# An x product of an LSTM's input stream on the whole TensorE array instead of on its four column quarters

## The chip, the cores and the metric

The kernel runs on one core of one Trainium2 chip. A core has five engines that work side by side: PE (TensorE, the 128x128 matmul array, with its weight loads listed apart as PEld), DVE (VectorE), ACT (ScalarE), POOL (GpSimd) and SP (SyncE, which here issues transfers). The metric is the device time of one execution in microseconds (us), lower is better; it is given as the median of several runs. Beside it stands the profile of one execution, whose span runs from the first to the last instruction.

## The reference, cut to what matters

```python
x = x + lstm(x, h0=cond_1024, Wx, Wh, b)          # x: (32, 512, 512) = batch, steps, features

xW = jnp.einsum('ntd,dg->ntg', x, Wx) + b          # Wx: (512, 2048)
c = 0
for each of the 512 steps:
    a = xW[:, t] + prev_h @ Wh                     # Wh: (512, 2048)
    i, f, o = sigmoid(a[:, :H]), sigmoid(a[:, H:2H]), sigmoid(a[:, 2H:3H])
    g = tanh(a[:, 3H:])                            # H = 512
    next_c = f * prev_c + i * g
    next_h = o * tanh(next_c)
```

Everything is 32-bit float. There are two kinds of matrix work: x times Wx, which depends on no step before it, and h times Wh, of which step t needs the h of step t-1.

## The kernel before, in words

**The recurrent product.** In a step, `h_part` multiplies h (32 batch rows, held transposed in four pieces of 128x32) by Wh. The 32 batch rows are the stationary operand, so one matmul fills only 32 of the array's 128 columns. Four matmuls, one for each quarter j of the hidden units, are therefore put on the four column quarters of the array, each with the same 128x32 piece of h and its own 512 columns of Wh, writing partitions 32j to 32j+31 of a bank of PSUM (`gbank`). With four pieces of h that is 16 matmuls a step. The steps up to 468 are done so; after that the banks are split in halves and no part of the stream is left.

**The stream of x products.** For steps 18 to 497, x times Wx is done ahead of time, in 15 groups of 32 steps, by a fast matrix multiplication scheme of two levels: 26 products of sums of blocks (the slots of a group), each again split into 7 products (Winograd's form of Strassen's scheme). So there are 15 x 26 x 7 = 2730 *x products*. One x product has a left operand of 128x128 (x, or sums of blocks of x, in `ubuf`, `xs0` or the tile `r1`) and a right operand of 128x256 (sums of blocks of Wx, mostly in `vring`, which is loaded again and again from DRAM), and it adds a 128x256 result to a bank of PSUM (`xbank` or `bbank`). ACT and DVE take the results out to `cbuf` and add them up, and SP stores them to DRAM, from where each step loads its own row (`xw`).

`emit_matmuls` issues the x products. Before the change it cuts the left operand into four pieces of 32 columns and issues four matmuls, one on each column quarter, all with the same right operand. A call gets a number n of quarter products that are due; when fewer than four are left, it issues half a product (128 of the 256 columns), and the next call the other half.

**Other matmuls.** The first 18 steps and a few at the end have their x times Wx done plainly (`plain_block`, `plain_part`, `Tail.matmuls`), with 128x32 stationary operands on the column quarters. At the very beginning eight bf16 matmuls with 128x128 operands of zeros open the banks.

**What sets the order.** All instructions from step 20 on, and those before it in a first piece, are collected by `Plan`, which keeps PE's instructions in program order (recurrent product of step t, then the x products due in step t, then the recurrent product of step t+1) and simulates the other engines with a table of costs (`Plan.cost`) to choose the order in which DVE, ACT, POOL and SP issue theirs. `cell` does the gates on ACT and DVE between two recurrent products: sigmoids and tanh, the products, the new cell, its tanh, the new h, and its transpose into `ht`, which the next `h_part` waits for. All instructions are recorded through one helper, so every row of the profile has its line, L127; rows are told apart by their tiles.

Names in the rows: `gbank<-wh_sb,ht` is the recurrent product, `xbank` or `bbank` `<-vring,ubuf` (or `r`, `xs`, `cbuf` and others on the right) an x product. "128*32" is the part of the array that an instruction uses, rows by columns. A 32-bit matmul shows as two records in the trace, each with a weight load of its own: the 16 matmuls of a recurrent product are 32 records, an x product on the quarters 8.

Of the kernel before, what the change touches and what calls it, by code (L numbers as in the profile page):

```python
# [14 lines left out]
P = 128  # L15
B = 32
# [6 lines left out]
W = G * P  # L23
# [60 lines left out]
RIGHT = {1: 0, 5: 1, 3: 2, 6: 3, 2: 4, 7: 5, 4: 6}  # L84
# [22 lines left out]
class Plan:  # L107
# [70 lines left out]
    def cost(self, engine, op, out, ins):  # L178
        n = self.columns(out)
        if engine == "PE":  # L180
            need = (n * 4 / 2.4 + 5.26) / 4
            return need, need + self.PE_DEPTH
        if engine == "DVE":
            if op == "memset":
                return n, n
            took = 178 + 1.04 * n if op == "transpose" else 155 + 1.04 * n
            return took - 80, took
        if engine == "ACT":
            took = (185 + 0.78 * n) if op == "activation" else (150 + 0.86 * n)
            return max(took - 120, 105.0), took  # L190
        if engine == "POOL":
            return 478.0, 478.0
        return 430.0, 0.0
# [19 lines left out]
    def flush(self):  # L213
# [23 lines left out]
        cost = [self.cost(o[0], o[1], o[3], o[4]) for o in ops]  # L237
        moved = [self.dma_time(o[3], o[4][0]) if "dma" in o[1] else (0, 0.0, "") for o in ops]
        horizon = sum(c[0] for c, o in zip(cost, ops) if o[0] == "PE")
        late = [0.0] * n  # L240
        after = horizon
        for i in range(n - 1, -1, -1):
# [6 lines left out]
            if e == "PE":  # L249
                v = min(v, after - cost[i][0])  # L250
                after = v
            late[i] = v
        self.problem = ops, preds, succs, cost, moved
        order, ready = self.listed(late)
        for move in MOVES:
# [14 lines left out]
    def shaken(self, late, seed, lo, hi, spread, engines):  # L270
# [4 lines left out]
        ]  # L275

    def simulate(self, ops, preds, succs, cost, moved, late, expect):
        n = len(ops)
        engines = ("PE", "DVE", "ACT", "POOL", "SP")
# [110 lines left out]
def kernel(  # L390
# [11 lines left out]
    nc = Plan(tc.nc)  # L402
# [278 lines left out]
    def group(g):  # L681
        if g not in groups:
            groups[g] = Group(g)
        return groups[g]
# [105 lines left out]
    def u_block(gr, i):  # L790
        if i < 2 * MB:
            q = XROWS.index(i // 2)
            assert gr.summed[q] == 4, (gr.g, i)
            return pairs_at(PLACES[gr.g % 2][q])[:, i % 2]
        return None
# [32 lines left out]
    def left_of(gr, s, r):  # L828
        b = u_block(gr, U_OF[s])
        return ubuf[:, gr.u[U_OF[s]], LEFT[r]] if b is None else b[:, 1 + LEFT[r]]  # L830

    def left_done(gr, s):
        u_used(gr, U_OF[s])
# [47 lines left out]
    def emit_matmuls(n):  # L881

        while n > 0 and pos[0] < 4 * len(items):
            i, q = divmod(pos[0], 4)
            row, slot, r = items[i]
            gr, s = group(slot // R), slot % R
            xb = xbank[slot % 5]
            if q == 0 and any(f in finished for f in needs(slot, r)):
                if wait_at_end[0]:
                    return  # L890
                evacuate()
            if r == 2:
                dst = bbank[:, slot % 2 * HW : (slot % 2 + 1) * HW]
            elif r in (5, 3):
                dst = xb[:, HW:W]
            else:
                dst = xb[:, 0:HW]
            start = q == 0 and (r == 2 or (r == 1 and s not in BIAS_OF))
            size = 4 if q == 0 and n >= 4 else 2
            cols = slice(q * HW // 4, (q + size) * HW // 4)  # L900
            for j in range(4):
                nc.tensor.matmul(
                    dst[j * B : (j + 1) * B, cols],
                    left_of(gr, s, r)[:, j * B : (j + 1) * B],
                    right_of(row, slot, RIGHT[r])[:, cols],
                    start=start,
                    stop=True,
                    skip_group_check=True,
                )
            pos[0] += size  # L910
            n -= size
            if pos[0] % 4 == 0:
                finished.append((slot, r))
                if r == 4:
                    left_done(gr, s)
                    if slot < HELD:
                        (free_u if slot == 1 else free_c).extend({1: (6, 7), 2: (V_OF[2],), 3: (V_OF[3],)}.get(slot, ()))

    def right_of(row, slot, k):
        if slot >= HELD:  # L920
            return vring[:, row % 3, k]
        return v_parts(V_OF[slot])[2] if k == 6 else v_parts(V_OF[slot])[k % 2][:, k // 2]

    def needs(slot, r):
        if r == 1:
            return ((slot - 5, 4),)
        if r == 2:
            return ((slot - 2, 2),)
        return {5: (), 6: ((slot, 5),), 3: ((slot, 5),), 7: ((slot, 3),), 4: ((slot, 7),)}[r]
# [29 lines left out]
    def evacuate():  # L959
        while wqueue and len(free_c) < sum(r == 5 for _, r in finished):  # L960
            w_op(True)
        for slot, r in finished:
            gr, s = group(slot // R), slot % R
            xb = xbank[slot % 5]
            if r == 5:
                gr.have[s, "c"] = take(free_c)
                t = buf_of(gr.have[s, "c"])
                nc.scalar.copy(t[:, 0:4:3], xb.rearrange("p (n c) -> p n c", n=2))
                continue
            if r in (1, 6):  # L970
                continue
            t = buf_of(gr.have[s, "c"])
            if r == 2:
                add(t[:, 0], bbank[:, slot % 2 * HW : (slot % 2 + 1) * HW], t[:, 0])
                room["dve"] -= cost_dve(256)
            elif r == 3:
                nc.scalar.copy(t[:, 1], xb[:, 0:HW])
                add(t[:, 1], xb[:, HW:W], t[:, 1])
                room["dve"] -= cost_dve(256)
            elif r == 7:  # L980
                add(t[:, 3], xb[:, 0:HW], t[:, 3])
                room["dve"] -= cost_dve(256)
            else:
                nc.scalar.copy(t[:, 2], xb[:, 0:HW])
                gr.have[s] = gr.have.pop((s, "c"))
                ready(gr, s)
        finished.clear()
# [92 lines left out]
    def v_parts(i):  # L1080
        if i < 8:
            return r1[:, i, 1:4], r2[:, i, 0:3], r2[:, i, 3]
        return split_parts(vroom[vt[i]])
# [318 lines left out]
    with tc.manual_schedule():  # L1402
# [8 lines left out]
        for q in range(2):  # L1411
            cols = slice(q * P, (q + 1) * P)
            nc.sync.dma_start(out=r1[:, 0:4, 1, cols], in_=first[:, :, 1, cols])
        nc.sync.dma_start(out=r1[:, 0:4, 0], in_=first[:, :, 0])
        for c in range(1, 4):
            ko, ki = divmod(c, 2)
            if c == 1:
                load_early(1, 1, 2)
            nc.sync.dma_start(
                out=r1[:, 4 * ko : 4 * ko + 4, 2 * ki : 2 * ki + 2].rearrange("p j s c -> p j (s c)"),  # L1420
# [5 lines left out]
            out=wh_sb[:, k].rearrange("p j c -> p (j c)"), in_=wh[:, k * NJ * W : (k + 1) * NJ * W]  # L1426
# [60 lines left out]
        for t in range(T):  # L1487
# [19 lines left out]
            if HEAD + 4 <= t < HEAD + 4 + 3 * len(V_DIRECT):  # L1507
                s, d = divmod(t - HEAD - 4, 3)
# [15 lines left out]
            if t < HEAD_STEPS:  # L1524
# [22 lines left out]
                for i, (kind, m, cs) in enumerate(chunks):  # L1547
# [16 lines left out]
                    else:  # L1564
# [22 lines left out]
                        if i == 0 and t + 1 in SEEDED and t + 1 != HEAD:  # L1587
                            seed_step(t + 1)
                        emit_matmuls(m)
                        room["dve"] += m * PROD / 4  # L1590
                        if i == late_cell:
# [21 lines left out]
            n = target  # L1613
# [19 lines left out]
            if t in LATE:  # L1633
                late_loads.pop(0)()
            emit_matmuls(n)
            load_v_ahead()
            if t == SPLIT - 1:
# [73 lines left out]
```

## Time and profile before

| | |
|---|---|
| time, median of 3 runs | 3058.33 us (3058.26 to 3058.35) |
| profiled execution: span from first to last instruction | 3056.5 us |
| what lies around the span | about 1.8 us, if the profiled execution took the median time |
| PE busy | 3050.1 us (100%), 43424 records |
| PEld busy | 1605.6 us (53%), 43424 records |
| DVE busy | 2362.2 us (77%) |
| ACT busy | 1479.6 us (48%) |
| POOL busy | 222.9 us (7%) |
| mean share of the 16 DMA engines | 75.5% in the main queue |
| granted TensorE clock | 1.000 |

The page does not give the profiled execution a time of its own apart from its span; 1.8 us is the difference to the median. A matmul's record begins when PE takes it up and its end is modelled, so records of successive matmuls overlap; how long PE needs for one is read from the distance between the starts of successive ones. A row of the timeline merges successive records of one kind: its start, the time to the end of the last of them, and their count. Busy time of an engine is the time covered by any of its records. Idle time stands with what ended it.

### The profile page before, as it was taken

How to read it: one execution, taken by the hardware profiler on the slowest of the kernel's cores; microseconds unless marked ns; L12 is line 12 of the kernel's file. 1: busy time of each engine (PE TensorE's matmuls, PEld its weight loads, DVE VectorE, ACT ScalarE, POOL GpSimd, SP SyncE). 2: the span in 40 equal slices, each digit the busy share in tenths (PEclk: the TensorE clock that was granted, in tenths of full speed). 3: DMA queues.
4: the chain of work that ended last, by engine and by line, in shares of the span. 5: the costliest groups of instructions: out<-in, count | busy, mean ns of one | idle time of the engine just before them, and what ended most of it. 6: DMA issues, size and time to landing. Idle time of an engine off the chain costs nothing.

```text
span 3056.5 us, 107859 instructions
## 1 busy us (share of the span) xinstructions
PE 3050.1 (100%) x43424; PEld 1605.6 (53%) x43424; DVE 2362.2 (77%) x6518; ACT 1479.6 (48%) x5511; POOL 222.9 (7%) x473
## 2 busy tenths in 40 slices
PE   9999999999999999999999999999999999999999
PEld 6774444444444555555555555555555555555666
DVE  8678787787878878787787877878778787787765
ACT  2345445454444544545445454454544545444554
POOL 0000000000000000000000000000000000000000
PEclk9999999999999999999999999999999999999999
DMA  9889877787877778778787787877777778788630
GB/s 352 288 281 291 265 255 256 236 265 231 273 242 248 260 237 268 247 239 273 228 271 237 245 267 238 264 242 250 256 246 252 250 250 262 244 259 273 206 98 20
DMA packets 321428, 753.92 MB, mean 247 GB/s; under 512 B 51104, under 2 KB 106400, under 8 KB 320416
## 3 DMA queue, kind: packets, MB, share of 16 engines
q1 hardware_dynamic: 320784, 747.02, 75.5%
q8 instruction: 342, 5.60, 0.8%
q14 instruction: 158, 1.29, 0.1%
q10 hardware_dynamic: 144, 0.01, 0.0%
HBM read 565.68 MB, written 184.29 MB: 245 GB/s over the span
## 4 chain that ended last, share of the span: by engine, by line
PE 99%; DVE 0%; DMA 0%; ACT 0%; issue 0%; SPq 0%; DVEq 0%
PE gbank L127 56%; PE xbank L127 38%; PE bbank L127 6%; DMA r<-in_L_cond_Wx_dram 0%; DVE prod L127 0%; ACT s L127 0%; DVE s L127 0%; SPq L127 0%; DVE hbuf L127 0%; DVE ht L127 0%; ACT tanh_c L127 0%; ACT vring L127 0%; DVE vring L127 0%; ACT cbuf L127 0%; ACT r L127 0%
## 5 line engine op out<-in xcount | busy, mean ns | idle before, releaser
L127 PE MATMUL gbank<-wh_sb,ht 128*32 128x512 f32 x14912 | 1695.2, 592 | 0.3
L127 PEld LDWEIGHTS gbank<-wh_sb,ht 128*32 128x32 f32 x14912 | 537.9, 110 | 820.9 <-issue 713.0
L127 ACT ACTIVATE s<-gbank 128x64 f32<-128x64 f32 (+2 forms) x1920 | 331.2, 257 | 1209.6 <-PE gbank L127 1208.0
L127 PE MATMUL xbank<-vring,ubuf 128*32 128x256 f32 (+1 forms) x13584 | 848.0, 368 | 0.0
L127 PEld LDWEIGHTS xbank<-vring,ubuf 128*32 128x32 f32 x13584 | 512.6, 110 | 305.6 <-issue 137.5
L127 DVE TENSOR_TENSOR prod<-s 128x128 f32<-128x128 f32 (+2 forms) x1093 | 296.9, 278 | 469.4 <-ACT s L127 464.8
L127 POOL TENSOR_TENSOR oc<-xnat,ht 128x128 f32<-128x128 f32 x469 | 222.7, 475 | 2642.7 <-DVE ht L127 1292.1
L127 ACT ACTIVATE tanh_c<-s 128x64 f32<-128x64 f32 (+1 forms) x921 | 236.8, 258 | 190.0 <-DVE s L127 185.7
L127 ACT COPY cbuf<-xbank 128x256 f32<-128x256 f32 (+1 forms) x696 | 289.2, 439 | 38.7 <-PE xbank L127 34.0
L127 ACT COPY gbank<-xw 128x512 f32<-128x512 f32 (+1 forms) x486 | 285.2, 589 | 0.2
L127 DVE STREAM_TRANSPOSE ht<-hbuf 128x64 f32<-128x64 f32 (+1 forms) x921 | 226.9, 246 | 65.1 <-DVE hbuf L127 1.8
L127 DVE TENSOR_TENSOR s<-prod 128x64 f32<-128x64 f32 (+1 forms) x1007 | 227.4, 226 | 34.1
L127 DVE TENSOR_TENSOR cbuf<-xbank,cbuf 128x256 f32<-128x256 f32 x462 | 180.8, 409 | 46.3 <-ACT cbuf L127 42.6
L127 DVE TENSOR_TENSOR cbuf<-cbuf 128x1024 f32<-128x1024 f32 x172 | 209.5, 1222 | 0.6
L127 PE MATMUL xbank<-vring,r 128*32 128x256 f32 (+1 forms) x3216 | 207.5, 357 | 0.0
L127 PE MATMUL xbank<-vring,xs 128*32 128x256 f32 (+1 forms) x3120 | 200.9, 356 | 0.0
L127 DVE TENSOR_TENSOR hbuf<-o,tanh_c 128x64 f32<-128x64 f32 (+1 forms) x921 | 190.2, 207 | 3.7 <-ACT tanh_c L127 3.4
L127 ACT COPY r<-xbank 128x256 f32<-128x256 f32 (+1 forms) x414 | 176.3, 439 | 15.7 <-PE xbank L127 13.8
L127 PE MATMUL bbank<-vring,ubuf 128*32 128x256 f32 (+1 forms) x2600 | 183.2, 342 | 0.0
L127 PEld LDWEIGHTS xbank<-vring,r 128*32 128x32 f32 x3216 | 120.5, 110 | 81.5 <-issue 47.4
L127 ACT ACTIVATE o<-gbank 128x128 f32<-128x128 f32 (+1 forms) x508 | 154.7, 305 | 0.0
L127 PEld LDWEIGHTS xbank<-vring,xs 128*32 128x32 f32 x3120 | 116.1, 110 | 62.4 <-issue 23.5
(178 smaller groups left out, 2290.4 us busy)
## 6 DMA issues: line engine op xcount, KB each, us to landing
vring<-vdram SPq DMA_DIRECT2D x310, 896.0 KB, 5.8
xw<-xwd SPq DMA_DIRECT2D x1920, 64.0 KB, 4.4
xwd<-cbuf SPq DMA_DIRECT2D x140, 512.0 KB, 4.3
xwd<-r SPq DMA_DIRECT2D x83, 512.0 KB, 4.5
out_dram<-oc SPq DMA_DIRECT2D x255, 128.0 KB, 3.8
xnat<-in_x_dram SPq DMA_DIRECT2D x63, 512.0 KB, 5.2
xs<-in_x_grouped_dram SPq DMA_DIRECT2D x45, 512.0 KB, 4.9
vring<-vdram SPq DMA_DIRECT2D x33, 512.0 KB, 5.1
```

The lines of the kernel that those rows point to most:

```text
L127: self.plan.add(self.name, op, lambda: call(*args, **kw), out, rest)
```

## The change

`emit_matmuls` issues one matmul for an x product (or half product), with the whole 128x128 left operand as the stationary operand and all 128 partitions of the bank as output, where it issued four with 32 columns each. The columns of the right operand, the bank, the flags and the order stay. `Plan.cost` is told that such a matmul needs PE for four times as long as one of the four did, so that the planner sees the same sum for a product. The recurrent products, the plain products and the tail keep their 32 columns.

```diff
@@ class Plan: def cost
         n = self.columns(out)
         if engine == "PE":
-            need = (n * 4 / 2.4 + 5.26) / 4
+            need = (n * 4 / 2.4 + 5.26) / (1 if out.ap[0][1] == P and n < W else 4)
             return need, need + self.PE_DEPTH
@@ def emit_matmuls
             start = q == 0 and (r == 2 or (r == 1 and s not in BIAS_OF))
             size = 4 if q == 0 and n >= 4 else 2
             cols = slice(q * HW // 4, (q + size) * HW // 4)
-            for j in range(4):
-                nc.tensor.matmul(
-                    dst[j * B : (j + 1) * B, cols],
-                    left_of(gr, s, r)[:, j * B : (j + 1) * B],
-                    right_of(row, slot, RIGHT[r])[:, cols],
-                    start=start,
-                    stop=True,
-                    skip_group_check=True,
-                )
+            nc.tensor.matmul(
+                dst[:, cols],
+                left_of(gr, s, r),
+                right_of(row, slot, RIGHT[r])[:, cols],
+                start=start,
+                stop=True,
+                skip_group_check=True,
+            )
             pos[0] += size
             n -= size
```

On DVE, ACT, POOL and SP the lists of instructions are the same before and after, in the same order; only PE's differs. A row gives the bank and the operands, the shape of the output (partitions by columns) and how many such matmuls follow one another; `xbank_66` to `xbank_70` are the five xbanks, `gbank_72` and `gbank_73` the two gbanks, `ht_96` and `ht_97` the two buffers of h, `xs_79` is xs0 and `r_74` is r1.

PE around two recurrent products in the middle of the program, before:

```order
L127 MATMUL xbank_66<-vring,xs_79 32x256 x4
L127 MATMUL xbank_70<-vring,ubuf 32x256 x4
L127 MATMUL gbank_73<-wh_sb,ht_96 32x512 x16
L127 MATMUL xbank_70<-vring,ubuf 32x256 x4
L127 MATMUL xbank_69<-vring,ubuf 32x256 x8
L127 MATMUL xbank_68<-vring,ubuf 32x256 x4
L127 MATMUL bbank<-vring,ubuf 32x256 x4
L127 MATMUL xbank_67<-vring,ubuf 32x128 x4
L127 MATMUL gbank_72<-wh_sb,ht_97 32x512 x16
```

The same place now:

```order
L127 MATMUL xbank_66<-vring,xs_79 128x256
L127 MATMUL xbank_70<-vring,ubuf 128x256
L127 MATMUL gbank_73<-wh_sb,ht_96 32x512 x16
L127 MATMUL xbank_70<-vring,ubuf 128x256
L127 MATMUL xbank_69<-vring,ubuf 128x256 x2
L127 MATMUL xbank_68<-vring,ubuf 128x256
L127 MATMUL bbank<-vring,ubuf 128x256
L127 MATMUL xbank_67<-vring,ubuf 128x128
L127 MATMUL gbank_72<-wh_sb,ht_97 32x512 x16
```

Every x product is one matmul of 128 output partitions where it was four of 32, at the same place; the recurrent products between them stay at 16 matmuls of 32 partitions, so the shape changes twice in every step. The half product (128 columns) ahead of the second recurrent product is halved as before.

PE in one of the early steps, where pieces of plain products (`gbank<-r,xnat`) stand between the x products, now:

```order
L127 MATMUL bbank<-r_74,xs_79 128x256
L127 MATMUL gbank_72<-r_74,xnat 32x256 x8
L127 MATMUL xbank_67<-ubuf,xs_79 128x256
L127 MATMUL xbank_66<-vring,ubuf 128x256
L127 MATMUL gbank_72<-r_74,xnat 32x256 x8
```

Here the shape changes at each plain piece too. Over the whole program the x products are 2506 matmuls of 128x256 and 448 of 128x128 (224 products in halves), and going down PE's list the shape goes from 32 to 128 partitions 479 times and as often back again.

## The prediction

> **What bounds the kernel now.** I read the page first: the busy line, the clock's slices, the main transfer queue (packets, MB, share of the 16 DMA engines), and the chain that ended last.
>
> ```profile
> PE 3050.1 (100%) x43424; PEld 1605.6 (53%) x43424; DVE 2362.2 (77%) x6518; ACT 1479.6 (48%) x5511; POOL 222.9 (7%) x473
> PEclk9999999999999999999999999999999999999999
> q1 hardware_dynamic: 320784, 747.02, 75.5%
> PE 99%; DVE 0%; DMA 0%; ACT 0%; issue 0%; SPq 0%; DVEq 0%
> ```
>
> PE sets the end alone: it is covered for 3050.1 of the 3056.5 us of the span and is 99% of the chain, at the full clock. A busy PE need not be a PE at its best rate, so the second view is PE's timeline over one step in the middle, with shapes kept apart; I take the distance between successive starts as the cost.
>
> ```profile
> 1502.49 3.64 PE L127 MATMUL gbank<-wh_sb,ht 128*32 128x512 f32 x32
> 1505.93 1.29 PE L127 MATMUL xbank<-vring,ubuf 128*32 128x128 f32 x24
> 1507.01 0.64 PE L127 MATMUL xbank<-vring,r 128*32 128x256 f32 x8
> 1507.44 0.64 PE L127 MATMUL bbank<-vring,r 128*32 128x256 f32 x8
> 1507.87 0.64 PE L127 MATMUL xbank<-vring,ubuf 128*32 128x256 f32 x8
> 1508.30 3.65 PE L127 MATMUL gbank<-wh_sb,ht 128*32 128x512 f32 x32
> 1511.74 0.64 PE L127 MATMUL xbank<-vring,ubuf 128*32 128x256 f32 x8
> ...
> 1608.15 0.43 PE L127 MATMUL bbank<-vring,ubuf 128*32 128x128 f32 x8
> 1608.37 3.64 PE L127 MATMUL gbank<-wh_sb,ht 128*32 128x512 f32 x32
> ```
>
> An x product (8 records: four quarters, two passes) takes 0.43 us from start to start, so a pass of four quarters over 256 columns takes about 0.216 us. A recurrent product of 8 passes over 512 columns takes 3.44 us, 0.43 a pass. Half an x product takes 0.22 us, 0.11 a pass. So a pass costs by its columns, about 0.84 ns each, almost nothing is fixed, and no gap stands between an x product and a recurrent product on either side. PE is full, and what this change adds to or takes from PE's own time goes straight to the end.
>
> The third view is who waits for h, since the stream between two recurrent products also covers the chain of ACT and DVE that makes the next h.
>
> ```profile
> 1506.19 0.68 ACT L127 ACTIVATE s<-gbank 128x128 f32<-128x128 f32 x4 [3.21 <-PE gbank L127]
> 1507.88 0.24 DVE L127 STREAM_TRANSPOSE ht<-hbuf 128x64 f32<-128x64 f32 x1
> ```
>
> The first half of h is there at 1508.12 (1507.88 + 0.24); the recurrent product starts at 1508.30. So the chain is about 0.18 us ahead of PE in this step. It starts when a recurrent product ends: anything that lengthens PE's work behind that point gives it more room, and a PE that got faster by more than this would wait here.
>
> **The change, part by part.** *Removed and added on PE.* Each of the 2730 x products loses four matmuls and gets one, 256 columns wide; 224 of them go in two halves, so there are 2506 whole matmuls and 448 halves, and with two passes each 5012 + 896 = 5908 passes. A pass still has to stream the same columns: four quarters stream theirs side by side, and the whole array streams them once. The only rows of before that show the array used whole are the opening's (the group, its place in the timeline, and the first matmul on quarters behind it):
>
> ```profile
> L127 PE MATMUL xbank<-zeros 128*128 128x512 bf16 x5 | 2.3, 634 | 0.0
> ...
> 1.81 2.34 PE L127 MATMUL xbank<-zeros 128*128 128x512 bf16 x5
> 5.22 0.32 PE L127 MATMUL gbank<-r,xnat 128*32 128x128 f32 x4 [0.64 <-DVE gbank L127]
> ```
>
> Five of these, 634 ns each as recorded, cover 2.34 us in the timeline, so the four distances between starts are (2.34 - 0.634) / 4 = 0.427 us for 512 columns: 0.83 ns a column, what a quarter pass in 32 bits takes. It is bf16, so it bounds the pass only loosely. I take 0.216 us for a whole pass of 256 columns in 32 bits, as now, and so 0 us for the streaming.
>
> *The weight load.* A pass on the quarters loads 4 x 32 columns; now it loads 128 in one piece. What a load of 32 costs when nothing covers it is seen early, where PE had stood still for data (groups between 9.05 and 9.3 us, then two groups of the whole span):
>
> ```profile
> L127 PE MATMUL gbank<-r,xnat 128*32 128x256 f32 x4 | 0.4, 403 | 0.1
> L127 PE MATMUL xbank<-vring,ubuf 128*32 128x256 f32 x12240 | 799.9, 379 | 0.0
> L127 PEld LDWEIGHTS xbank<-vring,ubuf 128*32 128x32 f32 x13584 | 512.6, 110 | 305.6 <-issue 137.5
> ```
>
> The first four matmuls after that pause are 403 ns instead of 379: 24 ns for 32 columns. One piece of 128 columns, at the same rate through one door, is an estimate of 4 x 24 = 96 ns. Today a load starts as the matmul ahead of it on the same quarter starts and costs nothing (0.216 us a pass is streaming alone). 96 ns is below the 216 ns of a whole pass and the 110 ns of a half, so I take 0 for it within the stream. Bounds: 0, and 96 ns in each of the 5908 passes.
>
> *The change of shape.* Today every matmul from 5 us on uses the quarters. Afterwards the array goes from quarters to whole 479 times and back as often. No row of before shows what that costs: the only such change is ahead of the row at 5.22 us, and a wait for DVE (0.64 us) covers it. I bound a pair of changes from rows. *Stagger*: four quarters of a pass do not start together.
>
> ```profile
> 1505.50 0.64 PE L127 MATMUL gbank<-wh_sb,ht 128*32 128x512 f32 x4
> L127 PE MATMUL gbank<-wh_sb,ht 128*32 128x512 f32 x14912 | 1695.2, 592 | 0.3
> ```
>
> The last pass of a recurrent product covers 0.64 us where one record is 592 ns, so its last quarter starts about 48 ns after its first. A matmul on the whole array needs the last one done: 48 ns for a pair, even if nothing else is lost. I see nothing that takes it below 0 (the other side is a rival below). *Flight*: if the array has to be empty before it is divided in another way, each change also waits until the last matmul is through. A record lasts 592 ns where the next may start after 429 (3.44 us / 8), or 379 where the next may start after 216: 163 ns in both. ACT starts on the bank at 1506.19, 0.05 us after that record's end at 1506.14, so at most 163 + 50 = 213 ns. *Load*: if the next weights cannot come in ahead either, 96 ns on the way to the whole array and 24 ns back.
>
> So a pair costs 48 ns at the low end (23 us in all), and at the high end 48 + 2 x 213 + 96 + 24 = 594 ns (285 us). I take stagger and flight, with the loads under the flight, since 96 and 24 ns are shorter than 163: 48 + 163 + 163 = **374 ns**. It is nearest to the rows in which a load overlaps the matmul ahead of it. 479 x 0.374 = 179 us.
>
> By the Trainium skill (TensorEngine Tiling, Tiling Modes, Key Properties) a change of the tiling mode, as against a change of the tile alone, drains TensorE. No run here shows that yet; it gives no duration, and the sum by it is the one above.
>
> *Moved, and the other engines.* Nothing moves: DVE, ACT, POOL and SP have their lists unchanged, all transfers included, and no wait is added. PE signals ACT at the same products, later by what the step grew. The first change of a step falls behind the end of the recurrent product, while ACT already works, so the chain that makes h gains that time as slack. The second falls between the stream and the next recurrent product, when h is already there (0.18 us ahead, and more now), so it is not hidden by a wait for h. Both add in full. DVE at 77% and the transfers at 75.5% only get more time for a step.
>
> *Sum.* 3056.5 + 0 (stream) + 0 (loads) + 179 (changes of shape) = 3235.6 us of span; with the 1.8 us around it (the median of 3058.33 less the span) **3237 us**, 5.9% slower.
>
> **The rivals.**
>
> *Shape costs only the stagger.* The array takes the 128-column matmul as soon as its quarters are free, and loads ahead. For it: the gapless neighbours and loads ahead within the quarters. Against: there the division never changes. 479 x 0.048 = 23 us: 3081.
>
> *The whole-array load is exposed in each pass.* Then each of 5908 passes costs 96 ns more, 567 us, and with the changes of shape 3058 + 567 + 179 = 3804. Against: loads on one quarter overlap the matmul on the same quarter now. A dearer stream of another kind belongs here (a whole-array pass in 32 bits at twice 0.216 us would add 5908 x 0.2 = 1.2 ms); the opening's 0.83 ns a column speaks against it, weakly because it is bf16.
>
> By the Trainium skill (TensorE: Matmul & The Clock Gate, Part 3, The mechanism) weight loads overlap matmuls in flight only when their row groups differ. Here all use all four row groups, and the 0.216 us pass with a 110 ns load record under it contradicts that for quarters; for the whole array no row decides.
>
> *Not slower: a pass gets cheaper.* One instruction replaces four. A pass of 512 columns takes 429 ns and one of 256 takes 216, so the columns alone take 213 and about 2.5 ns are fixed for four instructions. Should that fixed part go away and the array change its shape for nothing, 5908 x 2.5 ns = 15 us are gained: 3043. It decides only if a pair of changes costs less than 15 / 479 us = 31 ns, below the stagger of 48. What would hold it back is the wait for h, with only 0.18 us of room, but 0.03 us a step is within that.
>
> That the change does not do what it says is excluded by PE's list of instructions.
>
> **How the numbers follow.** The forecast with its variants (flight or load exposed, 80 to 285 us; the low one is 48 + 96 + 24 = 168 ns a pair) 0.62; stagger only 0.20; dearer passes 0.08; the gain 0.05; costs that cancel to within the bound 0.05. About 0.2%, 6 us, is what a measurement of this kernel can tell from no change. The range goes down to 3072, a little under the stagger alone, and up to 3330, near the high end of a pair (3058 + 285 = 3343); it leaves out the dearer passes, the gain and no change. Slower: 0.62 + 0.20 + 0.08 = 0.90; within 0.2% 0.05; faster 0.05.
>
> **What would show it.** In PE's timeline of the changed kernel: an x product still 0.43 us from start to start, in two records of 379 ns (right), or above 0.6 (dearer passes). Between the last x product and the recurrent product behind it 0.43 + about 0.16 us, and about 0.2 us between the last recurrent pass and the first x product beyond its 0.43. PE's idle before these rows, or records that are stretched, must come to about 0.37 us a step, and steps that took 5.8 us now should take about 6.2. The weight loads ahead of a change tell which variant it is: if they begin with the matmul ahead of them, they are covered; if they begin only behind the gap, they are part of it. ACT's and DVE's busy times should stay. The forecast is wrong if the neighbours stay gapless (then 3081 or less) or if the stream itself stretches.

## The result and the profile after

The changed kernel takes 3218.77 us (median of 4 runs, 3218.55 to 3219.15) where the kernel before took 3058.34 us on the same chip (median of 4): a ratio of 1.0524, 95% interval [1.0509, 1.0539]. That is 160.4 us slower; the prediction said 3237 us, with a range from 3072 to 3330. The changed kernel's profiled execution has a span of 3217.3 us.

The busy line of the page, the clock, the main transfer queue and the chain, for the changed kernel:

```profile
PE 3211.4 (100%) x25700; PEld 1665.0 (52%) x25700; DVE 2363.0 (73%) x6518; ACT 1491.5 (46%) x5511; POOL 222.4 (7%) x473
PEclk9999999999999999999999999999999999999999
q1 hardware_dynamic: 320784, 747.02, 70.5%
PE 100%; DVE 0%; DMA 0%; ACT 0%; issue 0%; DVEq 0%
```

PE has 17724 fewer records and is still covered from end to end at the full clock. DVE is busy for 2363.0 us and ACT for 1491.5, within 1% of before. So the 160 us are in PE's own time, and they cannot be found in its busy share: the records are modelled, and they bridge the short gaps that follow. The distances between starts show them. PE's timeline of one step follows (start, time to the end of the last record, count). A row runs on as long as bank and operands stay the same and shows the shape of its first record, so the row at 1603.45 is four whole products and, last, a half:

```profile
1602.15 0.61 PE L127 MATMUL gbank<-wh_sb,ht 128*32 128x512 f32 x4
1602.69 0.49 PE L127 MATMUL bbank<-vring,ubuf 128*128 128x128 f32 x2
1603.02 0.60 PE L127 MATMUL xbank<-vring,r 128*128 128x256 f32 x2
1603.45 2.11 PE L127 MATMUL xbank<-vring,ubuf 128*128 128x256 f32 x10
1605.49 3.64 PE L127 MATMUL gbank<-wh_sb,ht 128*32 128x512 f32 x32
1609.06 0.49 PE L127 MATMUL xbank<-vring,ubuf 128*128 128x128 f32 x2
```

- **Within the stream** nothing changed: the whole product of 1603.02 takes 0.43 us to the next start, in two records instead of eight.
- **To the whole array.** The last pass of the recurrent product starts at 1602.15; a record of it is 592 ns and the group ends after 0.61 us, so the last quarter starts about 0.02 us after the first. With 0.43 us for the pass it is done streaming at 1602.60, but the next matmul starts at 1602.69. I call these 0.09 us, in which PE takes nothing up, the *hold*. The half product behind it then takes 0.33 us (1602.69 to 1603.02) instead of 0.22: another 0.1 us, for a load that nothing covers (an *exposed* load).
- **Back to the quarters.** From 1603.45 the four products and a half should take 4 x 0.432 + 0.218 = 1.95 us, to 1605.40; the recurrent product starts at 1605.49, again 0.09 us late. It takes 3.57 us to the next start (1609.06) instead of 3.44: 0.09 for the hold at its end, 0.02 for the stagger, and 0.025 for its own first loads.

What the loads do stands in PEld's timeline of the same place:

```profile
1602.69 0.30 PEld L127 LDWEIGHTS bbank<-vring,ubuf 128*128 128x128 f32 x2 [0.84 <-issue]
1603.24 2.13 PEld L127 LDWEIGHTS xbank<-vring,ubuf 128*128 128x128 f32 x10
1605.49 0.16 PEld L127 LDWEIGHTS gbank<-wh_sb,ht 128*32 128x32 f32 x8
```

The load for the first product on the whole array (here a half product) begins at 1602.69, with its matmul, not with the matmul ahead of it: PEld had stood still for 0.84 us. Within the stream (second row) the loads of the next pass begin while a pass runs. The groups show the same, first in the window from 1605.4 to 1605.8 us around the change back (its second row is the half product ahead of it), then over the whole span:

```profile
L127 PE MATMUL gbank<-wh_sb,ht 128*32 128x512 f32 x4 | 0.6, 617 | 0.0
L127 PE MATMUL xbank<-vring,ubuf 128*128 128x128 f32 x2 | 0.4, 274 | 0.0
...
L127 PE MATMUL gbank<-wh_sb,ht 128*32 128x512 f32 x14912 | 1696.5, 595 | 0.0
L127 PE MATMUL bbank<-vring,ubuf 128*128 128x128 f32 x224 | 48.9, 300 | 0.0
L127 PEld LDWEIGHTS xbank<-vring,ubuf 128*128 128x128 f32 x3396 | 612.1, 190 | 280.5 <-issue 209.5
```

Behind the change the first four matmuls are 617 ns, 25 more than elsewhere; four of the 32 records of a recurrent product by 25 ns make the mean of all 14912 3 ns longer (595, before 592). The half products, of whose records every fourth stands behind a change, have a mean of 300 ns where the same shape had 273 on quarters: 27 x 4 = 108 ns for each exposed load (104 ns in the single record behind the change, 377 ns instead of 273; two of the other three are 2 ns longer).

Record by record, over all 479 pairs, the hold is nearly constant: 93 to 94 ns from the end of streaming to the next start (96 when the matmul ahead is a half product on the whole array), in both directions, whatever ran before (256 or 512 columns on quarters, 128 or 256 on the whole array). The exposed load is 104 to 105 ns to the whole array and 24 to 25 ns back. A pair is then 94 + 104 + 94 + 25 and 21 of stagger, **338 ns**, or 162 us for 479; the spans differ by 160.8.

By the Trainium skill (TensorEngine Tiling, Tiling Modes, Key Properties) changing the tiling mode drains TensorE. The trace agrees in so far as PE takes up no matmul for 94 ns at each change, and it adds a load that was not started ahead; that the 94 ns are the drain itself is not shown by any run.

### The profile page after: what moved, and what is told of

It reads as the page before. It is cut to its first block, busy times and chain, and to the rows that moved or that the text cites. A ratio compares the mean times of both kernels' runs of the same rounds, so it can differ in the third digit from the quotient of the medians.

```text
span 3217.3 us, 72401 instructions
## 1 busy us (share of the span) xinstructions
PE 3211.4 (100%) x25700; PEld 1665.0 (52%) x25700; DVE 2363.0 (73%) x6518; ACT 1491.5 (46%) x5511; POOL 222.4 (7%) x473
## 4 chain that ended last, share of the span: by engine, by line
PE 100%; DVE 0%; DMA 0%; ACT 0%; issue 0%; DVEq 0%
PE gbank L127 55%; PE xbank L127 39%; PE bbank L127 6%; DMA columns<-in_bias_columns_dram 0%; DVE gbank L127 0%; DVE bias_full L127 0%; DVE prod L127 0%; ACT vring L127 0%; DVE s L127 0%; DVE hbuf L127 0%; DVE vring L127 0%; DVE xbank L127 0%; ACT s L127 0%; DVEq L127 0%
## 5 line engine op out<-in xcount | busy, mean ns | idle before, releaser
L127 PEld LDWEIGHTS gbank<-wh_sb,ht 128*32 128x32 f32 x14912 | 438.8, 109 | 941.4 <-issue 830.2
L127 PE MATMUL xbank<-vring,ubuf 128*128 128x256 f32 (+1 forms) x3396 | 844.0, 377 | 0.0
L127 PEld LDWEIGHTS xbank<-vring,ubuf 128*128 128x128 f32 x3396 | 612.1, 190 | 280.5 <-issue 209.5
L127 PE MATMUL xbank<-vring,r 128*128 128x256 f32 (+1 forms) x804 | 205.9, 368 | 0.0
L127 PE MATMUL xbank<-vring,xs 128*128 128x256 f32 (+1 forms) x780 | 195.5, 362 | 0.0
L127 PEld LDWEIGHTS xbank<-vring,r 128*128 128x128 f32 x804 | 141.4, 190 | 85.5 <-issue 69.6
L127 PE MATMUL bbank<-vring,ubuf 128*128 128x256 f32 x650 | 177.4, 355 | 0.0
L127 PEld LDWEIGHTS xbank<-vring,xs 128*128 128x128 f32 x780 | 140.2, 190 | 51.7 <-issue 35.6
```

What stands on the lines that cost most here:

```text
L127: self.plan.add(self.name, op, lambda: call(*args, **kw), out, rest)
```

## The experiments

All four were timed beside the kernel before on one chip, where it took 3058.35 us (median of 7 runs, 3057.84 to 3060.50).

### One whole product a call

Only the second x product of each call is a whole one; the recurrent products keep quarter neighbours on both sides, and the change of shape falls between x products.

```diff
+        nth = 0
         while n > 0 and pos[0] < 4 * len(items):
...
-            nc.tensor.matmul(dst[:, cols], left_of(gr, s, r), ...)
+            nth += 1
+            width = P if nth == 2 else B
+            for j in range(P // width):
+                part = slice(j * width, (j + 1) * width)
+                nc.tensor.matmul(dst[part, cols], left_of(gr, s, r)[:, part], ...)
```

> Only the second x product of each call of emit_matmuls is one 128x128 matmul; the others stay on the column quarters. 500 whole products instead of 2730, but 500 pairs of changes of shape instead of 479. Theory (price per change of shape; by the changed kernel's trace a pair is 94 hold + 104 load to the whole array, 94 hold + 25 load back, 21 stagger = 338 ns): 3058 + 500 x 0.338 = 3227 us. Rival (price per whole product: the 160 us of the change over 2730 products are 59 ns each): 3058 + 500 x 0.059 = 3088 us.

Measured: 3226.0 us (3223.99 to 3226.31), ratio 1.0547 [1.0529, 1.0565]. The price goes by changes of shape: with 500 whole products instead of 2730 this kernel is slower still than the changed one. It is 167.7 us above the kernel before, or 335 ns a pair (331 by its fastest run); the changed kernel has 160.4 / 479 = 335 ns. The rival (3088) is out.

### Every second product whole

The same edit with `width = P if nth % 2 == 0 else B`.

> Every second x product of a call is one 128x128 matmul. 1422 pairs of changes of shape, 1422 whole matmuls. Theory (338 ns a pair): 3058 + 1422 x 0.338 = 3539 us. Rival (59 ns a whole product): 3058 + 1422 x 0.059 = 3142 us.

Measured: 3533.47 us (3533.03 to 3533.7), ratio 1.1552 [1.1535, 1.1569]: 475.1 us over 1422 pairs, 334 ns a pair, where the rival said 3142 us. PE's timeline shows a pair between single products:

```profile
1602.02 0.70 PE L127 MATMUL bbank<-vring,ubuf 128*128 128x256 f32 x2
1602.65 0.64 PE L127 MATMUL xbank<-vring,xs 128*32 128x256 f32 x8
1603.22 0.70 PE L127 MATMUL xbank<-vring,ubuf 128*128 128x256 f32 x2
1603.85 3.64 PE L127 MATMUL gbank<-wh_sb,ht 128*32 128x512 f32 x32
```

A whole product takes 0.63 us here (0.43, its load of 0.10, and the hold behind it), one on quarters 0.57 (0.43, 0.025, 0.02 and the hold): 1.20 us for the two, where two neighbours of one shape take 0.86. Three kernels with 479, 500 and 1422 pairs give 335, 335 and 334 ns; the number of whole products (2730, 500, about 1350: 1282 and 140 halves) plays no part.

### Halves of the array

Each x product is two matmuls with 64 columns of the left operand, on the two column halves, with the planner's cost to match. The edit is shown against the kernel before.

```diff
-            need = (n * 4 / 2.4 + 5.26) / 4
+            need = (n * 4 / 2.4 + 5.26) / (2 if out.ap[0][1] == 2 * B else 4)
...
-            for j in range(4):
-                nc.tensor.matmul(dst[j * B : (j + 1) * B, cols], left_of(gr, s, r)[:, j * B : (j + 1) * B], ...)
+            width = 2 * B
+            for j in range(P // width):
+                part = slice(j * width, (j + 1) * width)
+                nc.tensor.matmul(dst[part, cols], left_of(gr, s, r)[:, part], ...)
```

> Each x product is two matmuls of 64 columns on the halves of the array, 479 pairs of changes between halves and quarters. Theory (any change of the array's division holds PE 94 ns, and the load behind it costs about 26 ns for each 32 columns of one piece, so 52 to halves and 25 back, with 28 ns of stagger): 293 ns a pair, 3058 + 140 = 3199 us. Rival 1 (the load behind a change to another shape is 104 ns whatever its width): 3058 + 479 x 0.345 = 3223 us. Rival 2 (only the undivided array needs the hold): stagger alone, 3058 + 13 = 3071 us.

Measured: 3194.86 us (3194.46 to 3196.43), ratio 1.0446 [1.0430, 1.0461]: 136.5 us, or 285 ns a pair. PE's timeline:

```profile
1602.41 1.08 PE L127 MATMUL xbank<-vring,ubuf 128*64 128x256 f32 x8
1603.33 0.60 PE L127 MATMUL bbank<-vring,ubuf 128*64 128x256 f32 x4
1603.76 0.60 PE L127 MATMUL xbank<-vring,ubuf 128*64 128x256 f32 x4
```

A product on halves takes the same 0.43 us within the stream. The first two behind the change take 0.92 (1602.41 to 1603.33), 0.05 more than 0.86, for the exposed load. Record by record it is 51 ns for 64 columns, between 25 for 32 and 104 for 128, so it goes in proportion to the columns of a piece, and the hold is 93 to 94 ns as before. So a change between quarters and halves holds PE too, and the hold does not come from the use of the whole array; a change between halves and the whole was not run. Both rivals (3223 and 3071) are out.

### The old cost in the planner

The matmuls of the change, with `Plan.cost` as it was, so that the planner takes an x product for a quarter of its time. PE's list is the changed kernel's; DVE, ACT and SP issue in another order in some places.

```diff
-            need = (n * 4 / 2.4 + 5.26) / (1 if out.ap[0][1] == P and n < W else 4)
+            need = (n * 4 / 2.4 + 5.26) / 4
```

> The matmuls of the change with the planner's old cost (it takes an x product for a quarter of its time): PE's list is the changed kernel's, DVE's, ACT's and SP's orders differ in some places. Theory (PE alone sets the end, the orders of the others only matter if they make PE wait): 3219 us, up to 3240 if h or a buffer comes late in some steps. Rival (part of the 160 us comes from how the planner orders the others, so another order moves the time by tens of us): 3190 or above 3260 us.

Measured: 3227.4 us (3227.32 to 3229.02), ratio 1.0553 [1.0537, 1.0568], 8.6 us above the changed kernel and within the theory's range. The two profiled spans differ by about 10 us (3227.2 and 3217.3). The view of PE's waits names most of it (us in total, times, longest); behind the dots stands all that the same view of the changed kernel has, two waits of the opening:

```profile
PE gbank L127 <- DVE ht L127: 3.0, 3, 2.2
PE xbank L127 <- DVE ht L127: 1.8, 2, 1.5
PE xbank L127 <- ACT cbuf L127: 1.8, 1, 1.8
PE xbank L127 <- ACT o L127: 1.2, 1, 1.2
...
PE gbank L127 <- DVE zeros L127: 1.0, 1, 1.0
PE gbank L127 <- DVE gbank L127: 0.5, 1, 0.5
```

These 7.8 us are waits that the changed kernel does not have. They fall near the start: the 21st recurrent product in `gbank` already starts about 10 us later than in the changed kernel, and the last instruction ends no more than that later. So the order that the planner makes is worth 8 to 10 us when its costs are wrong by this much, and with the costs of the change this view has 1.5 us of waits, all in the opening: the 160 us are no matter of order.

## Why the prediction was right, and where its terms were not

**The total and its cause held.** PE sets the end alone; the streaming of an x product costs the same on the whole array (0.43 us); a load of 128 columns is covered within the stream; the price is paid at changes of shape and goes straight to the end. The forecast was 179 us for 479 pairs, the runs showed 160.4: 374 ns a pair against 335. That the time goes by the pair was shown with three different counts of pairs.

**The split of a pair was wrong, in three terms that partly cancel.** That the sum came out only 36 ns too high was in good part luck: the flight was 138 ns too long and the stagger 27, and the loads were 129 ns too short.

| term of a pair | predicted | measured |
|---|---|---|
| stagger | 48 ns | 21 ns |
| array held ("flight"), twice | 163 + 163 ns | 94 + 94 ns |
| loads | 0, under the flight | 104 + 25 ns |
| sum | 374 ns | 338 ns by records, 335 by time |

- *Flight.* The prediction took the whole part of a record beyond the next start, 163 ns, as the time until the array is empty. The next start comes 94 ns after streaming, 69 ns ahead of the modelled end. The record's end is a model; it bounded the hold (0 to 213 ns) but is no measure of it.
- *Loads.* They were taken as covered because loads overlap the matmul ahead of them in the rows of before that it showed. That is so only as long as the division stays. Ahead of a change the load begins behind the hold, together with its matmul, and all of it is exposed. The sizes were near: 96 and 24 ns predicted as exposed durations, 104 and 25 measured.
- *Stagger.* The 48 ns go back to an earlier recurrent product that had waited for h: its first quarter had its load covered while those of the other three were not, and the passes behind it keep the distance. Behind a change all four loads are exposed alike, and the quarters start 7 ns apart.

**The rivals.** *Stagger only* (3081) fell with the first gap in the timeline. *Dearer passes* (3804) fell with the 0.43 us of a product within the stream, and the first two experiments exclude any price by the product. *A cheaper pass* (3043) is not seen: a pass of 256 columns takes 0.216 us with one instruction as with four. As forecast, waits for h took up almost none of the added time (1.6 of 162 us, shown below): in the step of the timeline the first half of h is there at 1604.76 (1604.52 + 0.24) and the recurrent product starts at 1605.49. The row for it is in DVE's timeline of the changed kernel:

```profile
1604.52 0.24 DVE L127 STREAM_TRANSPOSE ht<-hbuf 128x64 f32<-128x64 f32 x1
```

By the Trainium skill (TensorE: Matmul & The Clock Gate, Part 3, The mechanism) a load overlaps matmuls in flight only when their row groups differ. Here it does so with all row groups in use, on quarters, halves and the whole array alike (load records of 110, 137 and 190 ns under passes of 216 ns), as long as the division stays the same; the measurement decides against that sentence taken alone. The same section also names a background weight buffer as a way to load ahead, which no run here tells apart.

**The room for h in the kernel before.** The prediction found no gap ahead of a recurrent product and gave h 0.18 us of room. Both were true of the steps that it showed, but not of all, as PE and DVE of the kernel before show at another step:

```profile
1654.20 1.51 PE L127 MATMUL xbank<-vring,ubuf 128*32 128x256 f32 x24
1655.42 0.25 DVE L127 STREAM_TRANSPOSE ht<-hbuf 128x64 f32<-128x64 f32 x1 [0.46 <-DVE hbuf L127]
1655.82 1.07 PE L127 MATMUL gbank<-wh_sb,ht 128*32 128x512 f32 x8
```

Three x products from 1654.20 take 1.30 us, to 1655.50, but the recurrent product starts at 1655.82, 0.15 us behind the end of the row that makes h. So a start 0.18 us behind h has only about 0.03 us to spare, and the faster pass of the third rival, 0.03 us a step, would have used all of it. By the distances between starts, nine of the 466 recurrent products in `gbank` waited so, for 1.6 us in all; the modelled records hide these gaps. In the changed kernel none does: even the two whose h came latest, 0.15 us ahead of the start, begin 93 ns behind the streaming, which is the hold alone.

**Open.** What the 94 ns consist of was not separated. The parts of a pair come to 338 ns and the times to 334 or 335. The 1.6 us that the kernel before lost to waits for h, and the changed kernel does not, are 3 ns for each of 479 pairs and are of the size of this difference. No version faster than the kernel before came out of this: with one division from 5.22 us on, the kernel before has no hold at all, and no pass became cheaper on a wider one.

## What to carry to other kernels

On a full TensorE, choose one division of the array for everything that alternates closely, even if some operands would fit a wider one in a single instruction: here the stream costs the same on quarters, halves and the whole, and each pair of changes costs 335 ns (285 with halves). Count the changes of shape in the instruction list and multiply; the number of instructions saved (17724 records here) is worth nothing while PE streams without gaps. And read PE's cost from the distances between starts: its busy share stayed at 100% while it lost 160 us.

## What had not been expected of the hardware

- The hold at a change of division is constant to a few ns: 93 to 96 ns after the streaming ends, for quarters to whole, quarters to halves and both ways back, behind matmuls of 128, 256 or 512 columns, by the single records of four kernels.
- Weights are not loaded ahead across a change of division: the load begins with its matmul, and costs 25, 51 and 104 ns for pieces of 32, 64 and 128 columns in 32 bits, about 0.8 ns a column.
